# A two-layer gated cross-attention kernel on Trainium2: both fixed TensorE orders laid out anew

## The chip, the cores and the metric

The kernel runs on one core of a Trainium2 chip. A core has five engines that run at the same time, each its own stream of instructions in a fixed order: TensorE (PE, matrix products and transposes; its weight loads are a row of their own, PEld), VectorE (DVE), ScalarE (ACT), GpSimd (POOL) and SyncE (SP), which here issues most of the transfers. Data lies in SBUF (128 partitions); products are written to PSUM, which has eight banks. The metric is the device time of one execution in microseconds (us); lower is better.

## What is computed

Eight sequences (batches) of 256 rows by 512 columns pass through two layers; each layer is a gated cross-attention to a context and a gated feed-forward. Cut to what matters:

```python
x = x + tanh(g_xattn[0]) * attention0(layernorm(x), ctx)   # 16 heads of 32, causal, keys = values = ctx
x = x + tanh(g_ffn[0])   * ffn0(layernorm(x))              # ternary weights, silu(gate)*up over 2048,
                                                           # rms_norm of the result, ternary projection
x = x + tanh(g_xattn[1]) * attention1(layernorm(x), ctx)   # q and k linear + rms_norm, v linear, 16 heads,
                                                           # then an output product
x = x + tanh(g_ffn[1])   * ffn1(layernorm(x))
def ffn1(x):
    h  = x * rsqrt(mean(x*x) + EPS) * w_norm
    gv = act_quant(h) @ ternary(w_gv).T                    # act_quant: 8 bits, one scale for a row
    value, gate = split(gv)
    return x + act_quant(value * silu(gate)) @ ternary(w_out).T
```

The second scale in `ffn1` (that of `value * silu(gate)`) needs the largest value of a whole row of 2048, so nothing of the last product can start before all of a row tile's gated values are there.

## The kernel before

*Stages.* A row tile is 128 rows; there are 16, two for a batch. From 0 to about 260 us the kernel makes layer 0's ternary weights, layer 1's keys and values (kept in DRAM) and the attention of the first two batches. From about 260 to 775 us a block for each batch runs layer 0's feed-forward, and beside it the layer-0 attention of batch 2 and on, then the layer-1 attention of the first two batches, and POOL and ACT make layer 1's ternary weights. From about 799 to 1243 us a block for each batch runs layer 1's feed-forward and the layer-1 attention of the batches that follow.

*Two kinds of order.* PE's order in the last two of these stages is written out by hand: a job `at(b, (k, step))` stands at place `b + k/16` of a line of blocks, `timeline` sorts the jobs and calls them, and `pe.held` ties every product to the one before. A place is called a step in what follows (16 steps are a block of one batch, and a job at step 23.2 runs at step 7.2 of the next block). The order of DVE, ACT and POOL is not written out: it is chosen when the program is built, from a simulated timeline, and then stands fixed in the program.

*PSUM.* `pair` has two buffers, each two banks wide, shared in turn by the scores (`s`), `turned`, `back`, `nt` and `ut`. Of the rest, layer 0 has bank `o` (one buffer), `gu` (two) and `y` (one); layer 1 has `o` (one), `gu` (two) and `py` (one). A new user of a one-buffer bank waits until the last reader is done.

*Layer 0's block* (`Feed0`). `hidden` runs 32 products into `gu` for each of 8 chunks of each of two row tiles (steps 0 to 15), then ACT's tanh (`h`), two products on DVE, ACT's copy `hs`, its rest on DVE or POOL, ACT's square, and POOL's sum `acc`. `project` follows `LAG = 3` steps later with 4 products into `y`. `factor` makes the mean square of a row tile by one product `ssq` (in bank `o`) from `acc`; `add` scales `y` by it and adds it to `x`. `ready` normalises the two tiles of the next batch (`norm`) and turns them by a DMA (`xT<-yp`).

*Attention, in both layers.* `ready` normalises and turns the rows (in layer 1 also two products `lin` and their norm, for the queries). `looks` are six jobs: four `scores` (of four heads each), whose maxima DVE takes (`nm`, L415 or L407), `parts` (POOL splits the maxima into three bf16 parts, `mz` and `nmr`, ten instructions) and `shift` (PE transposes them, `nt`). `weighs` are eight jobs: `exps` (scores again, transposed, with the maxima subtracted on PE; ACT's exponentials `p`, L481) and `weigh` (products into bank `o`; ACT copies them to `oT`, L505; POOL adds up the sums, L508), in the order exps0, exps1, weigh0, exps2, weigh1, exps3, weigh2, weigh3. `done` divides by the sums and adds. Layer 0 (`Attention0.done`) transposes `oT` into `back` and the sums into bank `o`, DVE inverts them and multiplies, and adds to `x`, for both tiles in one job; the product is written back into `oT`. In layer 1 (`Attention1.done`) DVE inverts the sums (L1008), `divide` spreads them by products into `inv` (two, in banks `o` and `py`), which DVE multiplies into `oT` (L1022), and `add(i)` runs the output product `proj` (banks `o` and `py`) and adds it to `x`. L256 is the line that records every matmul, L259 every transpose.

*Layer 1's block* (`Feed1`, one object for each row tile). `first` is the batch's even tile, `second` its odd one. `ready` is `norm` (POOL and DVE make `yr`, `z`, the row's scale and the quantized `zq`; its rows are also called rs_r, y, z) and a DMA that turns it (`zT<-zq`). `glu(k)`, for k of 0 to 7, is 8 products into `gu`, and ACT's copy to `gv` (L1186); after each second one come ACT's tanh `t`, DVE's `t`, `u` and the maximum `umax`. The first tile's eight are steps 0 to 7, the second's steps 8 to 15 (there called glu 8 to 15). `done` is five jobs: `quantize` (DVE takes the maximum of `umax`, and the scale `s`, by five small instructions around L1206; ACT's two `u<-u,magic,s`, L1232; POOL's two `uq`), two DMA turns, and two `project` of eight products each into `py` (the even tile's uses bank `o`, the odd one's bank `py`), after which DVE adds the result to `x` (L1223) and it is stored to DRAM. For the very last tile `last` does the same with transposes on PE (`ut`) in place of the DMA turns.

The places of all these jobs in a block of layer 1 are the tuples of the diff's last part; steps above 16 belong to the block after the one they are counted from.

## Time and profile before

| | us |
|---|---|
| three runs | 1246.83, 1250.46, 1248.93 (median 1248.93) |
| the profiled execution | 1244.33 |
| its span, first to last instruction | 1242.6 |

| stretch of the span, us | PE busy | DVE | ACT | POOL | granted PE clock |
|---|---|---|---|---|---|
| 0 to 260: weights, keys and values, first attention | 217.25 | 191.28 | 128.69 | 92.59 | 0.91 |
| 260 to 775: layer 0's blocks | 471.16 | 284.94 | 242.30 | 251.52 | 0.99 |
| 775 to 799: hand-over | 19.70 | 17.86 | 3.56 | 20.83 | 1.00 |
| 799 to 1243: layer 1's blocks | 405.73 | 328.90 | 236.61 | 185.05 | 0.98 |

All times of the tables are of the profile's windows view; the clock is a share of full speed. PE's busy time is not time at its peak: products are pipelined, and a row of the timeline that says "x16" is sixteen of them in one stretch. In the waits view a row such as "PE inv <- DVE x: 7.4, 5, 1.7" says that PE stood idle before an `inv` product 7.4 us in all, in five waits, the longest 1.7, and that the last thing to be ready was DVE's `x`. A wait shorter than the rounding of the view, or of several causes, is put down to the one that came last. In a timeline row the columns are the start, the duration, engine, line, operation, output and inputs with their shapes, and in brackets what the instruction had waited for.

### The profile page before, as it was taken

Reading aid. Unit: us, or ns where it says so; the run is one execution under the profiler, and the core shown is the slowest. Engines: PE = TensorE matmul, PEld = TensorE weight load, DVE = VectorE, ACT = ScalarE, POOL = GpSimd, SP = SyncE. Lnnn points to the kernel's source line nnn. Section 1 sums busy time; section 2 is a strip of 40 time slices with the busy share of each in tenths; the row PEclk is TensorE's granted clock in tenths of the full one; section 3 lists DMA queues with packets and bytes.
Section 4 is the critical chain, followed back from the end, with each engine's and each line's share of the span. In section 5 each row is a group of like instructions: output and inputs, shape, how many; then the busy total and the mean of one; then the engine's idle time right before and its main releaser. Section 6 shows DMA issues by size and latency. Waiting matters only on the chain.

```text
span 1242.6 us, 29878 instructions
## 1 busy us (share of the span) xinstructions
PE 1113.8 (90%) x12466; PEld 725.7 (58%) x12565; DVE 823.0 (66%) x1776; ACT 611.2 (49%) x1108; POOL 550.0 (44%) x821
## 2 busy tenths in 40 slices
PE   7988977799999897888999998899999999999976
PEld 3444433577777666666666775455555555555553
DVE  5677797764656455375654645777777777768684
ACT  3446547356575533433344453356464645464663
POOL 3333224353343556465564424826263535424250
PEclk9998888899999998999999999999999999999998
DMA  8343424622333233223222002311212121211231
GB/s 320 127 137 114 158 85 119 221 61 96 120 99 118 64 99 82 82 70 95 84 76 66 19 18 71 109 52 31 64 35 60 35 61 35 61 35 31 39 51 43
DMA packets 101767, 103.91 MB, mean 84 GB/s; under 512 B 61312, under 2 KB 72576, under 8 KB 101632
## 3 DMA queue, kind: packets, MB, share of 16 engines
q1 hardware_dynamic: 98608, 97.01, 26.6%
q10 hardware_dynamic: 3024, 4.98, 1.3%
q8 instruction: 98, 1.61, 0.5%
q14 instruction: 37, 0.30, 0.1%
HBM read 72.09 MB, written 15.73 MB: 71 GB/s over the span
## 4 chain that ended last, share of the span: by engine, by line
PE 29%; DVE 27%; POOL 12%; ACT 8%; issue 5%; DMA 1%; POOLq 0%; DVEq 0%; ACTq 0%
PE gu L256 10%; PE o L256 5%; PE s L256 5%; DVE nm L415 4%; PE y L256 3%; PE py L256 2%; DVE u L1193 2%; DVE h L843 2%; POOL acc L850 2%; DVE ln_st L277 2%; POOL w L957 2%; DVE t L1191 2%; DVE h L842 2%; POOL q L961 2%; DVE umax L1194 2%
## 5 line engine op out<-in xcount | busy, mean ns | idle before, releaser
L256 PE MATMUL gu<-xT,gu 128*128 128x128 f16 x4096 | 254.9, 221 | 11.7 <-DVE h L843 8.3
L256 PEld LDWEIGHTS <-gu 128*128 128x128 bf16 x4096 | 237.7, 99 | 42.2 <-issue 18.6
L850 POOL TENSOR_TENSOR acc<-acc,h 128x256 f32<-128x256 f32 x112 | 83.5, 745 | 130.6 <-ACT h L848 127.0
L256 PE MATMUL gu<-gv,zT 128*128 128x256 fp8e4 x1024 | 131.4, 274 | 10.9 <-ACT gv L1186 6.4
L1186 ACT COPY gv<-gu 128x512 f32<-128x512 f32 x128 | 74.0, 585 | 116.2 <-PE gu L256 108.3
L256 PEld LDWEIGHTS <-zT 128*128 128x128 bf16 x1024 | 96.0, 98 | 57.4 <-issue 36.7
L845 ACT CAST hs<-h 128x256 f16<-128x256 f32 x128 | 51.7, 404 | 147.0 <-DVE h L843 146.6
L842 DVE SCALAR_TENSOR_TENSOR h<-h,gu 128x256 f32<-128x256 f32 x128 | 53.3, 416 | 102.3 <-ACT h L841 97.0
L256 PE MATMUL y<-pr,hs 128*128 128x512 bf16 x413 | 113.5, 383 | 6.9 <-issue 1.4
L270 POOL TENSOR_TENSOR rs_r<-rs_t,mhalf 128x1 f32<-128x1 f32 (+1 forms) x88 | 60.7, 694 | 129.0 <-DVE rs_t L268 108.1
L481 ACT ACTIVATE p<-s 128x768 f32<-128x768 f32 (+1 forms) x128 | 109.8, 908 | 15.1 <-PE s L256 15.1
L415 DVE TENSOR_REDUCE nm<-s 128x4 f32<-128x1024 f32 x64 | 75.8, 1217 | 33.9 <-PE s L256 33.9
L848 ACT ACTIVATE h<-h,hid 128x256 f32<-128x256 f32 x112 | 56.6, 507 | 70.1 <-POOL hs L295 46.6
L508 POOL TENSOR_TENSOR oT<-oT 128x256 f32<-128x256 f32 x48 | 35.3, 735 | 124.3 <-ACT oT L505 124.1
L256 PE MATMUL s<-qT,kT 32*128 32x256 f32 (+1 forms) x1024 | 78.2, 377 | 2.5 <-DVE rs_t L268 1.1
L295 POOL TENSOR_TENSOR hs<-h,hs 128x256 f16<-128x256 f32 x64 | 44.5, 695 | 77.8 <-ACT hs L845 77.8
L841 ACT ACTIVATE h<-gu 128x256 f32<-128x256 f32 x128 | 48.5, 379 | 56.9 <-PE gu L256 56.7
L1191 DVE SCALAR_TENSOR_TENSOR t<-t,gv 128x512 f32<-128x512 f32 x64 | 46.4, 725 | 41.6 <-ACT t L1190 41.6
L256 PE MATMUL s<-kT,qT 32*128 32x256 f32 (+1 forms) x1024 | 68.9, 378 | 2.0 <-DVE nm L415 1.3
L407 DVE TENSOR_REDUCE nm<-s 128x2 f32<-128x256 f32 (+1 forms) x128 | 62.9, 551 | 11.6 <-PE s L256 11.3
L256 PE MATMUL o<-p,v 128*32 128x256 f32 (+1 forms) x1024 | 64.2, 370 | 5.8 <-DVE x L1223 5.6
L256 PEld LDWEIGHTS <-hs 128*128 128x128 f16 x512 | 45.6, 101 | 35.4 <-issue 4.7
(185 smaller groups left out, 2195.4 us busy)
## 6 DMA issues: line engine op xcount, KB each, us to landing
w<-in_gvT_dram SPq DMA_DIRECT2D x32, 512.0 KB, 3.8
w<-in_guT_dram SPq DMA_DIRECT2D x32, 256.0 KB, 3.0
w<-in_outT_dram SPq DMA_DIRECT2D x16, 512.0 KB, 3.6
cT<-in_cxT_dram SPq DMA_DIRECT2D x8, 512.0 KB, 4.9
x<-in_x_dram SPq DMA_DIRECT2D x16, 256.0 KB, 6.6
kT<-in_cxT_dram SPq DMA_DIRECT2D x8, 512.0 KB, 4.0
v<-in_cx_dram SPq DMA_DIRECT2D x8, 512.0 KB, 3.8
vd<-v SPq DMA_DIRECT2D x8, 512.0 KB, 5.3
```

What stands on the lines that cost most here:

```text
L256: return self.kept(nc.tensor.matmul(*args, **kwargs))
L270: nc.gpsimd.tensor_tensor(r[:, :n], t[:, :n], mhalf[:, :n], ALU.pow)
L407: nc.vector.tensor_reduce(nm[:, :, qb], s[j][:, :, at[qb] : at[qb] + to[qb]], AX.X, ALU.max, negate=True,)
L415: nc.vector.tensor_reduce(nm, s[j].rearrange("p r (q k) -> p r q k", q=2), AX.X, ALU.max, negate=True)
L481: exp[0] = nc.scalar.activation(self.p[j], s[j][:, :, 0:n], AF.Exp)
L841: block["A"] = nc.scalar.activation(h, gu[:, 0], AF.Tanh, scale=0.5 / UP0)
L842: nc.vector.scalar_tensor_tensor(h, h, 1.0, gu[:, 0], ALU.add, ALU.mult)
L845: nc.scalar.copy(hs[:, 0], h)
L848: nc.scalar.activation(sq, h, AF.Square, scale=hid[:, 1:2])
L850: block["P"] = nc.gpsimd.tensor_tensor(self.acc[i], self.acc[i], sq, ALU.add)
L1186: nc.scalar.copy(self.gv[:, :, k % 2, :], gu)
L1191: nc.vector.scalar_tensor_tensor(t, t, 1.0, g, ALU.add, ALU.mult)
```

## The change

It is a change of order, almost without any of work. In layer 0, `factor` moves from the place ahead of chunk 6's last products to the place of chunk 7's (same step as the last `project` of a tile), `ready` of the feed-forward from 12.4, 13.4 to 11.7, 12.7; the looks are spread over steps 3.3 to 14.6 (scores at 3.3, 6.2, 9.3, 12.4), weigh1 moves from 22.2 to 21.2, and `done` becomes two jobs, each with its tile's transposes; the sums are transposed and inverted in the first; the product goes to a new tile `w`, which takes a buffer of the ring `y` (four buffers), not back into `oT`. In layer 1, `weighs(late)` swaps exps3 and weigh2; `done` becomes five jobs (invert, two `divide`, two `add`); the second `project` of `first` moves from step 18.2 to 15.4 and of `second` from 24.2 to 23.2; the looks, the weighs, `lin`, and the norms of the next feed-forward move; for the last batch but one, both `project` of `second` (tile 13) move from 23.9 to 31.9, the end of the whole order.

```diff
@@ -78,8 +78,6 @@
 MP = 3
 
 LAG = 3
-
-AHEAD0 = 1
 
 YB = 4
 
@@ -513,7 +511,7 @@
-        def weighs(self):
+        def weighs(self, late=False):
 
 
             def exps(g):
@@ -526,6 +524,8 @@
                 if g + 1 < DC:
                     steps.append(lambda g=g: exps(g + 1))
                 steps.append(lambda g=g: self.weigh(g, ps.pop(g)))
+            if late:
+                steps[5:7] = steps[6], steps[5]
             return self.counted(self.nready + DC + 2, steps)
 
         def finish(self, steps):
@@ -554,36 +554,41 @@
             return self.counted(0, [load, norm, turn])
 
         def done(self):
-            def add():
-
-                t = pair((P, 2, D), name="back")
+
+            st = {}
+
+            def divide():
                 sums = bank("o", (P, 2, P), name="sums")
                 for i in range(2):
-                    rows = slice(i * P, (i + 1) * P)
-                    for c in range(DC):
-                        pe.transpose(
-                            t[:, i, c * P : (c + 1) * P], self.oT[:, c, rows], ident
-                        )
-                    pe.transpose(sums[:, i, :], self.sums[:, rows], ident)
-                inv = small.tile([P, 2, DC, 4], F32, tag="inv", name="inv", bufs=2)
+                    pe.transpose(sums[:, i, :], self.sums[:, i * P : (i + 1) * P], ident)
+                st["inv"] = small.tile([P, 2, DC, 4], F32, tag="inv", name="inv", bufs=2)
                 nc.vector.reciprocal(
-                    inv, sums.rearrange("p i (r g e) -> p i g r e", r=4, g=DC)[:, :, :, :, 0]
+                    st["inv"], sums.rearrange("p i (r g e) -> p i g r e", r=4, g=DC)[:, :, :, :, 0]
                 )
...
-                    reach(2 * self.b + i, 1)
-
-            return self.finish([add])
+                if i == 0:
+                    divide()
+                inv = st["inv"]
+                xt = xs[2 * self.b + i]
+                w = att.tile([P, D], F32, tag="y", name="w", bufs=YB)
+                nc.vector.tensor_tensor(
+                    w.rearrange("p (h c) -> p h c", h=NH),
+                    t[:, i, :].rearrange("p (h c) -> p h c", h=NH),
+                    inv[:, i].rearrange("p g r -> p (g r)").unsqueeze(2).broadcast_to([P, NH, HD]),
+                    ALU.mult,
+                )
+                nc.vector.scalar_tensor_tensor(xt, w, tg[:, 0:1], xt, ALU.mult, ALU.add)
+                reach(2 * self.b + i, 1)
+
+            return self.finish([lambda: add(0), lambda: add(1)])
 
     def load_w(pool, name, wT):
         w = pool.tile([P, DC, D], F32, tag=f"w{name}", name=f"w{name}", bufs=1)
@@ -872,7 +877,7 @@
-                if n % 8 == 7 - AHEAD0:
+                if n % 8 == 7:
                     self.factor(n // 8)
                 self.project(n % 8, self.hs.pop(n))
                 if n % 8 == 7:
@@ -1007,19 +1012,18 @@
             def invert():
                 nc.vector.reciprocal(self.oT[:, DC + 1, :], self.sums)
 
-            def divide():
-                for k in range(2):
-                    w = bank(("o", "py")[k], (P, 2, S), name="inv")
-                    for j in range(2):
-                        pe.matmul(
-                            w[:, j, :],
-                            lhsT=spread[:, 2 * k + j, :],
-                            rhs=self.oT[:, DC + 1, :],
-                            start=True,
-                            stop=True,
-                        )
-                    cols = self.oT[:, 2 * k : 2 * k + 2, :]
-                    nc.vector.tensor_tensor(cols, cols, w, ALU.mult)
+            def divide(k):
+                w = bank(("o", "py")[k], (P, 2, S), name="inv")
+                for j in range(2):
+                    pe.matmul(
+                        w[:, j, :],
+                        lhsT=spread[:, 2 * k + j, :],
+                        rhs=self.oT[:, DC + 1, :],
+                        start=True,
+                        stop=True,
+                    )
+                cols = self.oT[:, 2 * k : 2 * k + 2, :]
+                nc.vector.tensor_tensor(cols, cols, w, ALU.mult)
 
             def add(i):
                 xt = xs[2 * self.b + i]
@@ -1029,7 +1033,7 @@
                 nc.vector.scalar_tensor_tensor(xt, t, tg[:, 1:2], xt, ALU.mult, ALU.add)
                 reach(2 * self.b + i, 3)
 
-            return self.finish([invert, divide, lambda: add(0), lambda: add(1)])
+            return self.finish([invert, *(lambda f=f, k=k: f(k) for f in (divide, add) for k in range(2))])
 
     att1 = [Attention1(b) for b in range(B)]
     x2 = ctx.enter_context(tc.tile_pool(name="x2", bufs=1, side="right", reuse_waits="tile"))
@@ -1058,24 +1062,24 @@
 
 
 
-        jobs += at(0, *zip((-5.0, -4.0), feed0[0].ready()), (-4.5, *att0[1].done()))
+        jobs += at(0, *zip((-5.0, -4.0), feed0[0].ready()), *zip((-4.5, -4.4), att0[1].done()))
         for b in range(B):
             jobs += at(b, *((k, step) for k, step in enumerate(feed0[b].chunks())))
             if b == 0:
                 jobs += at(b, *zip((4.4, 5.4), feed0[1].ready()))
             elif b + 1 < B:
-                jobs += at(b, *zip((12.4, 13.4), feed0[b + 1].ready()))
+                jobs += at(b, *zip((11.7, 12.7), feed0[b + 1].ready()))
         for n, a in enumerate([*att0[2:], *att1[:2]]):
             if n < B - 2:
                 jobs += at(n, (-11.0, lambda n=n: rows(n + 2)))
-                jobs += at(n, *zip((-4.8, -2.4, 4.2 if n == 0 else 0.2), a.ready()))
+                jobs += at(n, *zip((-4.8, -2.4, 4.2 if n == 0 else 1.2), a.ready()))
             else:
-                jobs += at(n, *zip((-9.6, -7.6, -4.8, -3.7, -2.6, -2.5, 0.2), a.ready()))
-            jobs += at(n, *zip((*((5.4, 7.2) if n == 0 else (1.2, 5.2)), 9.2, 10.4, 10.8, 14.6), a.looks()))
+                jobs += at(n, *zip((-9.6, -7.6, -4.8, -3.3, -2.4, -2.3, 1.2), a.ready()))
+            jobs += at(n, *zip((*((5.4, 7.2) if n == 0 else (3.3, 6.2)), 9.3, 12.4, 12.6, 14.6), a.looks()))
             if a is not att1[1]:
-                jobs += at(n, *zip((15.3, 18.2, 19.2, 20.2, 22.2, 23.2, 24.2, 25.2), a.weighs()))
+                jobs += at(n, *zip((15.3, 18.2, 19.2, 20.2, 21.2, 23.2, 24.2, 25.2), a.weighs()))
             if n < B - 2:
-                jobs += at(n, (27.7, *a.done()))
+                jobs += at(n, *zip((26.6, 27.6), a.done()))
         pe.held = True
         timeline(*jobs)
     w0ctx.close()
@@ -1281,24 +1285,25 @@
         end = b == B - 1
         jobs += at(b, *((k, step) for k, step in enumerate(first.glus() + second.glus())))
 
-        far = {B - 1: (15.9, 15.9), B - 2: (15.95, 15.95), B - 3: (13.2, 17.3)}.get(b, (13.2, 18.2))
+        far = {B - 1: (15.95, 15.95), B - 2: (15.95, 15.95)}.get(b, (13.2, 15.4))
         jobs += at(b, *zip((7.4 if b == B - 2 else 8.6, 9.6, 9.8, *far), first.done()))
         if end:
             jobs += at(b, (16.0, second.last))
         else:
-            far = {B - 2: (23.9, 23.9), B - 3: (21.2, 22.2)}.get(b, (21.2, 24.2))
+            far = {B - 2: (31.9, 31.9), B - 3: (21.2, 22.2)}.get(b, (21.2, 23.2))
             jobs += at(b, *zip((17.4, 18.4, 18.6, *far), second.done()))
         if b >= 2:
 
-            late = 15.6 if b == 2 else 16.2
-            jobs += at(b - 3, *zip((3.6, 12.2, 12.5, 14.2, late, 16.5, 18.9), a.ready()))
-            jobs += at(b - 2, *zip((4.4, 6.4, 7.4, 9.3, 10.4, 14.1), a.looks()))
+            head = b == 2
+            turn, far = (11.25, 15.6) if head else (12.3, 17.2)
+            jobs += at(b - 3, *zip((3.6, turn, 12.5, 14.2, far, 17.5, 20.3), a.ready()))
+            jobs += at(b - 2, *zip((5.3, 7.3, 9.2, 11.3, 11.6, 14.1), a.looks()))
         if b >= 1:
-            steps = (-0.8, 0.6, 2.3, 2.5, 3.2, 3.4, 4.2, 5.0) if end else (-0.8, 1.2, 3.2, 3.4, 4.2, 5.6, 6.2, 7.2)
-            jobs += at(b - 1, *zip(steps, a.weighs()))
-        steps = (5.1, 6.9, 7.6, 8.2) if end else (7.3, 9.2, 10.2, 11.2)
+            steps = (-0.8, 0.6, 2.3, 2.5, 3.2, 3.4, 4.2, 5.0) if end else (-1.1, 0.2, 2.2, 3.2, 4.2, 6.2, 6.3, 8.2)
+            jobs += at(b - 1, *zip(steps, a.weighs(not end)))
+        steps = (5.1, 6.9, 6.9, 7.6, 8.2) if end else (8.3, 11.1, 11.15, 11.2, 12.2)
         jobs += at(b - 1, *zip(steps, a.done()))
-        for n, f in zip((7.7, 8.4) if end else (10.3, 13.0), (first, second)):
+        for n, f in zip((7.7, 8.4) if end else (11.35, 14.0), (first, second)):
             norm, turn = f.ready()
             jobs += at(b - 1, (n, norm), (n + 1.7, turn))
     timeline(*jobs)
```

What the change does to the other engines' order shows in the built programs, listed here for a steady block of layer 1 (numbers are the glu's; `oT(w3)` is the copy of the last weigh). ACT, from the last weigh on:

```text
before: oT(w3), gv7, u x2, gv8, t, gv9, gv10, t, ...
after:  gv7, t7, gv8, u x2, oT(w3), gv9, t9, gv10, gv11, t11, gv12, xT
```

DVE, from the first scores of the block on:

```text
before: nm x2, t, u, umax, reciprocal oT, amax, nm, amax, nm, s8i, s.., x<-py, oT*inv x2, t, u, ...
after:  nm x2, x<-py, t, u, umax, nm, amax, nm, amax, s8i, s, g, s, nm, t, reciprocal oT, nm, u, t,
        oT*inv, umax, oT*inv, u, umax, x<-proj
```

PE, jobs by glu step of the block, after (before: exps3 in step 5, weigh2 in 6, weigh3 in 7, `divide` in 9 beside the fourth scores, `add` in 10 and 11):

```text
14.9 exps0 | 0 exps1 | 1 lin1 | 2 weigh0 | 3 exps2 | 4 weigh1, turned | 5 py (second, 8 of 16), scores0
6 weigh2, exps3 | 7 py (second), scores1 | 8 weigh3 | 9 scores2 | 11 inv x2, proj0, scores3
12 proj1, turned y | 13 py (first, 8 of 16) | 14 nt, lin0 | 15 py (first)
```

POOL before has the parts (`mz`, `nmr`) of a batch together, ahead of the norm's y and z; after, the second norm's `rs_r`, `yr`, `z` stand ahead of and among them. In a block of layer 0, POOL before has the ten parts together and ahead of the norms' y; after, the norms' rs_r and y stand ahead of and among them. DVE there, after, from `ssq` of the second tile on:

```text
after:  nm x4, q, rs_t<-ssq, h, h, rgf, x<-y, reciprocal, hs, w, x, h, bn_stats, h, w, bn_aggr, x, h, bn_stats x3, h, ...
        nm x2 (the last maxima)
```

More of the change, by code (lines that the diff above doesn't have):

```diff
@@ L569, in add @@
                 nc.vector.reciprocal(
-                    inv, sums.rearrange("p i (r g e) -> p i g r e", r=4, g=DC)[:, :, :, :, 0]
+                    st["inv"], sums.rearrange("p i (r g e) -> p i g r e", r=4, g=DC)[:, :, :, :, 0]
                 )
-                for i in range(2):
-                    xt = xs[2 * self.b + i]
-                    w = self.oT[:, 2 * i : 2 * i + 2, :].rearrange("p c t -> p (c t)")
-                    nc.vector.tensor_tensor(
-                        w.rearrange("p (h c) -> p h c", h=NH),
-                        t[:, i, :].rearrange("p (h c) -> p h c", h=NH),
-                        inv[:, i].rearrange("p g r -> p (g r)").unsqueeze(2).broadcast_to([P, NH, HD]),
-                        ALU.mult,
-                    )
-                    nc.vector.scalar_tensor_tensor(
-                        xt, w, tg[:, 0:1], xt, ALU.mult, ALU.add
-                    )
-                    reach(2 * self.b + i, 1)
@@ L586, in done, with add @@
-            return self.finish([add])
+            def add(i):
+                if i == 0:
+                    st["t"] = pair((P, 2, D), name="back")
+                t = st["t"]
+                for c in range(DC):
+                    pe.transpose(
+                        t[:, i, c * P : (c + 1) * P], self.oT[:, c, i * P : (i + 1) * P], ident
+                    )
+                if i == 0:
+                    divide()
[10 more added lines that the diff above has]
+                reach(2 * self.b + i, 1)
@@ L1008, in invert @@
                 nc.vector.reciprocal(self.oT[:, DC + 1, :], self.sums)
-            def divide():
-                for k in range(2):
-                    w = bank(("o", "py")[k], (P, 2, S), name="inv")
-                    for j in range(2):
-                        pe.matmul(
-                            w[:, j, :],
-                            lhsT=spread[:, 2 * k + j, :],
-                            rhs=self.oT[:, DC + 1, :],
-                            start=True,
-                            stop=True,
-                        )
-                    cols = self.oT[:, 2 * k : 2 * k + 2, :]
-                    nc.vector.tensor_tensor(cols, cols, w, ALU.mult)
+            def divide(k):
[10 more added lines that the diff above has]
+                nc.vector.tensor_tensor(cols, cols, w, ALU.mult)
             def add(i):
```

## The prediction

> **What bounds the kernel now.** I read the page first (busy shares), then who waited for whom on TensorE (PE) in two stretches, then the timelines of VectorE (DVE) and ScalarE (ACT) in one block of layer 1, then the granted clock in short windows.
>
> ```profile
> span 1242.6 us, 29878 instructions
> PE 1113.8 (90%) x12466; PEld 725.7 (58%) x12565; DVE 823.0 (66%) x1776; ACT 611.2 (49%) x1108; POOL 550.0 (44%) x821
> ```
>
> PE is busy 90% of the span, and each engine runs its instructions in a fixed order. So the change cannot remove work from PE; it can only shorten or lengthen the holes in PE's row, 129 us in all. The waits of PE from 290 to 760 us (layer 0's feed-forward; columns: total us, times, longest):
>
> ```profile
> PE ssq L256 <- POOL acc L853: 6.8, 3, 3.6
> PE gu L256 <- DVE h L843: 6.3, 5, 1.6
> PE ssq L256 <- ACT oT L505: 5.5, 4, 2.3
> PE s L256 <- ACT p L481: 4.3, 7, 0.7
> PE gu L256 <- DMA xT<-yp: 3.3, 3, 1.6
> PE turned L259 <- ACT p L481: 2.0, 1, 2.0
> PE turned L259 <- POOL acc L850: 1.8, 1, 1.8
> PE back L259 <- DVE nm L407: 1.7, 3, 1.1
> ```
>
> The mean square `ssq` is the costliest single place (12.3 us). From 880 to 1180 us, five equal blocks of layer 1 (one and the same `s` product starts at 937.94 and 998.16, so a block lasts 60.2 us):
>
> ```profile
> PE inv L256 <- DVE x L1223: 7.4, 5, 1.7
> PE o L256 <- DVE x L1223: 4.5, 4, 1.2
> PE lin L256 <- DVE lin L696: 2.7, 4, 0.9
> PE gu L256 <- DMA zT<-zq: 1.2, 3, 0.5
> ```
>
> The first two are the one-buffer banks `py` and `o`: the next user waits until DVE has stored the feed-forward's product. The four make 15.8 us, 3.2 a block. What lies around them on DVE and ACT:
>
> ```profile
> 943.53 1.74 DVE L1008 RECIPROCAL oT<-oT 128x256 f32<-128x256 f32 x1
> 945.21 1.21 DVE L415 TENSOR_REDUCE nm<-s 128x4 f32<-128x1024 f32 x1
> 948.03 0.75 DVE L1223 SCALAR_TENSOR_TENSOR x<-py,g,x 128x512 f32<-128x512 f32 x1
> 948.69 0.68 DVE L1022 TENSOR_TENSOR oT<-oT,inv 128x512 f32<-128x512 f32 x1
> ```
> ```profile
> 942.05 0.59 ACT L505 COPY oT<-o 128x512 f32<-128x512 f32 x1 [0.61 <-PE o L256]
> 944.02 0.59 ACT L1186 COPY gv<-gu 128x512 f32<-128x512 f32 x1 [1.39 <-PE gu L256]
> 948.15 2.37 ACT L1232 ACTIVATE u<-u,magic,s 128x1024 f32<-128x1024 f32 x2 [3.54 <-DVE s L1206]
> ```
>
> The reader is to see the order: ACT copies the last `oT` and a `gv` before it waits 3.54 us for the quantizing scale `s`, and DVE's reciprocal is long done when PE comes to `inv`.
>
> **The change, part by part.**
>
> *Layer 1, what it removes.* `second`'s products end in step 23.2, not 24.2, so bank `py` is stored long before `inv`; `first`'s end in 15.4, not 18.2, three steps before the first weigh needs bank `o`; the two `lin` are three steps apart, not two; between the first `proj` and the next block's first `gu` PE now has some 17.9 us of work (before 15.7), so `zT` lands in time. All 3.2 us a block, for the six blocks with this order 19 us.
>
> *Layer 1, what it adds.* In the changed program's own order (listed in the section above) ACT's two `u` now stand ahead of the last `oT` and of glu 9's `gv`, and DVE's reciprocal behind `s` and behind `t` of glus 8 and 9. I add the chain up, from the end of `second`'s last products (step 7), by the rows of the timelines: DVE x 0.75; t, u, umax 3 x 0.69; nm 1.2, amax 0.1, nm 1.2; five small ones to `s` 0.7: 6.0 us. ACT u 2.37, oT 0.59, gv 0.59, tanh 0.72: 10.3. DVE t 0.69, reciprocal 1.74: 12.7. Only then can `inv` start. PE's own work in between: s 1.08, gu 0.98, weigh 1.86, gu 0.98, s 1.08, two gu 1.76: 7.7. So 5.0 us of wait, part of it already ahead of glu 11, because the `gu` bank has two buffers and glu 9's copy is stuck behind `u`. After the reciprocal DVE has nm 1.2, u 0.69, t 0.69 and the first multiplication 0.68 to do, 3.2 us; PE has 2.0 us of `inv`, then `proj` waits 1.2 (before, a whole glu stood between them). Together 6.2 us a block, 37 us in six; net of the 19 removed: +18. Queued behind ACT's wait for `s` are the last weigh's copy, POOL's sum of it and the two quantized halves `uq`; behind DVE's, the maxima of the third scores.
>
> *The clock.* Short matmuls between waits also cost clock:
>
> ```profile
> 1203.00:1206.00 3.00, 1.03 (x8) 1.00 0.22 44
> 1206.00:1209.00 3.00, 1.86 (x8) 0.52 0.66 126
> ```
>
> (columns: us, PE busy, granted clock.) After waits of 1.14 and 1.71 us around one `gu` the clock fell to half, and the 16 `py` after it took 5.46 us against 3.62 elsewhere: 1.84 lost. The other end is none: waits of 2.85 and 0.99 around 773 to 777 us left it at 1.00. The changed block has the first pattern (2.4, 2.3 and 1.2 us around 0.9 and 2.0 of work), so I take 1.8 a block, +11. The Trainium skill says otherwise: "TensorE: Matmul & The Clock Gate", in "Why this matters for your kernels", asks only that no single idle gap exceeds about 3 us. By it the clock would stay whole here and the sum below would be 11 us smaller; the row at 1206 has no gap above 1.8 us and fell all the same, so the row decides.
>
> *Layer 1, the last pair of batches.* The turned maxima `nt` come 7.9 us of PE work after the last scores; DVE and POOL need about 9 for them (nm 2.4, the first tile's norm rows 959 to 964 in between, parts 1.8). +2, between 0 and 4.
>
> *Layer 0.* In the first half of a block the scores stand a whole weigh behind the exponentials and `ssq` stands behind scores and 32 products, so `s<-p` 4.3 and `ssq<-oT` 5.5 go: -10. In the second half `ssq` of the second tile moves behind 32 more products and a `y` (2.0 + 0.85), which covers 2.9 of its longest wait of 3.6. But the fourth scores move from four steps ahead of `nt` to two. From the step of `ssq` on, DVE has, ahead of these last maxima: nm 1.95, q 0.70, three h pairs 2.7, x 0.75, inverse 0.35, hs 0.41, two w 1.3, two x 1.9, four bn_stats 2.5, small ones 0.9: 13.5; with q 0.7, its own nm 1.95 and some 1.2 of waiting it ends at 17.3. POOL then owes, in its new order, the norms' y (two pairs, 1.51 each), rs_r, acc 0.72, hs 0.67 and the parts (some 2.1): `mz` is done at about 21 without layer 1's weight quantizing beside it and 23.4 with it. PE is there at 17.2. So `nt` waits 3.8 twice and 6.2 twice, 20 us; the waits this absorbs (ssq 6.8, gu<-h 6.3, xT 3.3, turned 3.8, back 1.7) are 21.9. With one more fall of the clock (+2) and crumbs (+1): layer 0 gives -9. Ends: -20 if POOL lets the parts through, 0 if the absorbed waits come back.
>
> *Splitting `done` in two and its new tile `w`.* Same instructions, same sizes; `w` takes a buffer of ring `y`, whose other users are steps away. Nothing, hidden behind the 32 products between the halves (2.0 us against w 0.65 + x 0.95); without that cover 1.6 a block. Layer 0's first stage has the same products in slightly other order: 0. The hand-over at 773 us: `ssq` one `y` later, -1.
>
> *The end.* Tile 13's 16 products leave the place at 1208 to 1214.5 (0.95 wait, 5.46) for the hole ahead of the last transposes:
>
> ```profile
> 1231.58 1.26 PE L259 MATMUL ut<-ident_b,uq 128*128 128x128 bf16 x8 [3.87 <-DVE uq L1263]
> ```
>
> That saves 6.3. But DVE's store of them now stands ahead of the last t, u, umax: from the last gu, py 3.6 + x 0.75 + 2.07 + small 0.9 + ACT 0.73 + uq 0.43 = 8.5, against 7.3 before: +1.2, and 0.6 for ACT, which is nearly full there. -4.5, between -6 and 0.
>
> **The sum.** +18 +11 +2 -9 -1 -4.5 = +16.5. On the profiled execution, span 1242.6 and 1244.33 in all, that is 1260.8; the median of the runs lies 4.6 above it, 1248.93, so 1265.
>
> **The rivals.** *Faster:* the chain through `s` does not bind. Then layer 1 keeps its 19 us and pays only the wait of `proj` for the multiplication next to it (0.5 a block, 3); with layer 0, hand-over and end -14.5: -30, 1219. For it: DVE is idle 3 to 4 us a block (939.12 came after 3.43 of idling), so a store that comes a little earlier moves the whole chain. Against it: the order on ACT and DVE is fixed, and the chain has 5 us too much. It decides from where the new waits, clock and all, fall below 5.3 a block (3.2 removed, 12.5 gained elsewhere over six). *No change:* the chain holds, but the clock stays whole and layer 0 gives 15, its middle to good end: 18 + 2 - 15 - 1 - 4.5 = 0, 1249. *Slower still, by layer 0:* the waits of `nt` (over 3 us each) let the clock fall every time and `xT` is late as before; layer 0 gives nothing or loses: +28 to +35, about 1280. For it: 488 to 492 us, where 32 products took 3.62 us after a wait of 2.75. Against: the pause lets DVE and POOL catch up. *The change doesn't do what it says:* the weighing steps are even on PE alone; that is the forecast itself.
>
> **How the numbers follow.** Forecast 0.58, faster 0.20, no change 0.12, slower still 0.10. A difference of 0.3% (3.7 us) is about what runs of this kernel can tell. Ends of the costs: low, chain 1 us shorter and no clock +12, layer 0 -20, end -6, hand-over -1: -15, 1234; high, chain 1 us longer with clock +35, last pair +4, nothing elsewhere: +39, 1288. I leave out the outermost on both sides: 1236 to 1283.
>
> **What would show it.** In a block of layer 1: `inv` waiting for the reciprocal (L1010 or near) 2 us or more, a `gu` waiting for `gv` just before, `proj` waiting for DVE 1 us; ACT's `u` followed by the last `oT`; no wait of `o` or `inv` for x. In layer 0: no `ssq<-oT`, `nt` waiting for POOL's `mz` 3 to 6 us four times. At the end: no hole of 3.87. I am wrong if blocks of layer 1 last under 60 us.

## The result, and the profile after

The changed kernel takes 1324.15 us (median of four runs, 1323.47 to 1326.02), the kernel before 1247.88 beside it: a ratio of 1.0614 with a 95% interval of 1.0588 to 1.064. It is slower by 76 us, some 60 more than I had forecast. The first lines of the page of its profile:

```profile
span 1322.5 us, 29890 instructions
PE 1157.2 (88%) x12473; PEld 751.1 (57%) x12565; DVE 817.6 (62%) x1776; ACT 611.4 (46%) x1108; POOL 545.7 (41%) x821
```

DVE, ACT and POOL work about as long as before (823.0, 611.2, 550.0). PE's busy time grows by 43.4 us with the same products, and its holes by 36.5. The granted clock also falls more often: summed over windows of 1 us from 240 us to the end, what the clock lacks of full speed (1 less the granted share, times the time) is 13.7 us before, in 5 falls, and 58.0 after, in 23.

To place the loss I cut every span at the first product of layer 0's feed-forward (`gu<-xT`), at that of layer 1's (`gu<-gv`), and at the last store's sum:

| us | up to layer 0's first product | layer 0's blocks and hand-over | layer 1 to the last store |
|---|---|---|---|
| before | 232.7 | 566.5 | 439.7 |
| after | 240.7 | 585.2 | 492.8 |
| difference | +8.0 | +18.7 | +53.1 |

PE's busy time and holes in the last two columns, here to the end of the span, tell two losses of different kinds. In layer 0 the holes grow by 13.3 us (50.4 to 63.7) and the busy time by 5.5 (516.1 to 521.5); the clock lacks 16.3 us more there (25.2 against 8.9), but all four of its falls between 350 and 570 us begin while PE stands, so what it lacks is more than what it costs. In layer 1 the holes grow by 16.3 us (37.8 to 54.1) and the busy time by 36.8 (405.7 to 442.5); the clock lacks 25.9 us more (32.7 against 6.8), which leaves 10.9 of busy time that it does not account for.

The waits of PE in layer 0's part of the changed kernel (290 to 780 us):

```profile
PE nt L257 <- POOL mz L432: 27.5, 4, 8.7
PE s L254 <- DVE nm L405: 4.8, 10, 0.7
PE lin L254 <- DVE rs_t L266: 3.8, 1, 3.8
PE sums L257 <- DVE rs_t L266: 3.7, 3, 1.6
PE lin L254 <- DVE nm L413: 3.0, 1, 3.0
```

The old waits of `ssq` are gone from the list. In their place stands `nt`, four times 6.9 us on average, and behind it new names (`lin`, `sums`). One of the four, in the timeline of DVE, POOL and PE:

```profile
488.33 1.01 DVE L405 TENSOR_REDUCE nm<-s 128x2 f32<-128x256 f32 x2
489.65 1.51 POOL L288 TENSOR_SCALAR y<-x,ln_mv,rs_r 128x512 f32<-128x512 f32 x2
...
491.83 1.95 POOL L288 TENSOR_SCALAR y<-x,ln_mv,rs_r 128x512 f32<-128x512 f32 x2
493.75 0.61 POOL L425 TENSOR_SCALAR mz<-nm 128x16 bf16<-128x16 f32 x2
...
497.45 0.37 POOL L432 TENSOR_SCALAR mz<-nmr 128x16 bf16<-128x16 f32 x2
497.71 0.46 PE L257 MATMUL nt<-ident_b,mz 128*128 128x128 bf16 x2 [8.73 <-POOL mz L432]
```

The last maxima were done at 489.3. POOL made the norm's two pairs of `y` first and came to the parts 4.4 us later; the parts then took 4.1, and PE stood 8.73.

In layer 1, 900 to 1260 us, which holds five waits of `inv`:

```profile
PE inv L254 <- DVE oT L1013: 10.6, 5, 2.1
PE gu L254 <- ACT gv L1190: 9.7, 5, 1.9
PE s L254 <- ACT p L479: 8.1, 6, 2.1
```

The four lines of before (`inv` and `o` for `x`, `lin`, `zT`) are gone, as meant. The first two lines here are the chain of the prediction. One instance of it, DVE, ACT and PE in order of time:

```profile
1066.60 0.15 DVE L1210 TENSOR_TENSOR s<-s,back 128x1 f32<-128x1 f32 x1
1066.78 2.38 ACT L1236 ACTIVATE u<-u,magic,s 128x1024 f32<-128x1024 f32 x2 [3.21 <-DVE s L1210]
...
1069.06 0.56 ACT L503 COPY oT<-o 128x512 f32<-128x512 f32 x1
1069.53 0.58 ACT L1190 COPY gv<-gu 128x512 f32<-128x512 f32 x1
...
1071.50 1.75 DVE L1013 RECIPROCAL oT<-oT 128x256 f32<-128x256 f32 x1
...
1073.30 2.07 PE L254 MATMUL inv<-oT,spread 128*128 128x256 f32 x4 [2.11 <-DVE oT L1013]
```

ACT waits 3.21 us for the scale `s`, runs both `u`, and only then copies the last weigh; PE stands 1.93 for `gv` and 2.11 for the reciprocal. The third line, `s` for `p`, I had not seen coming. ACT alone, some 40 us earlier:

```profile
1020.30 0.58 ACT L1190 COPY gv<-gu 128x512 f32<-128x512 f32 x1 [1.22 <-PE gu L254]
1029.93 0.63 ACT L702 ACTIVATE junk<-lin 128x512 bf16<-128x512 f32 x1 [9.04 <-DVE lin L701]
1030.55 1.92 ACT L479 ACTIVATE p<-s 128x1024 f32<-128x1024 f32 x2
```
```profile
1026.22 0.69 DVE L1149 TENSOR_REDUCE amax<-z 128x1 f32<-128x512 f32 x1 [1.09 <-POOL z L1147]
...
1028.78 0.52 DVE L1154 TENSOR_SCALAR z<-z,s 128x512 f32<-128x512 f32 x1
1029.22 0.68 DVE L701 TENSOR_TENSOR lin<-lin,rqb 128x512 f32<-128x512 f32 x1
```

ACT idles 9.04 us before the square of `lin` (the sum of squares for the queries' norm), and the block's first exponentials are queued behind it. The square waits for DVE's bias sum of `lin` (L701), which stands in DVE's order behind the quantizing of the second norm (L1149 to L1154), although PE's product `lin` was done at 1024.2. The scores that want the exponentials' buffers wait 2.08 us, and the clock falls:

```profile
1029.00:1032.00 3.00, 0.92 (x7) 0.95 0.19 38
1032.00:1035.00 3.00, 3.00 (x25) 0.50 0.03 6
1035.00:1038.00 3.00, 3.00 (x12) 0.50 0.23 87
```

(stretch, its length, PE busy, granted clock, DMA share, GB/s.) For six microseconds PE is busy all the time at half speed. From 860 to 1180 us before, no window of 1 us fell below 0.99; after, 25.5 us are lacking between 861 and 1175.

### The profile page after: what moved, and what is told of

It reads as the page before. It is cut to its first block, busy times and chain, and to the rows that moved or that the text cites. A ratio compares the mean times of both kernels' runs of the same rounds, so it can differ in the third digit from the quotient of the medians.

```text
span 1322.5 us, 29890 instructions
## 1 busy us (share of the span) xinstructions
PE 1157.2 (88%) x12473; PEld 751.1 (57%) x12565; DVE 817.6 (62%) x1776; ACT 611.4 (46%) x1108; POOL 545.7 (41%) x821
## 4 chain that ended last, share of the span: by engine, by line
PE 33%; DVE 24%; POOL 13%; ACT 9%; issue 4%; DMA 0%; DVEq 0%; POOLq 0%; ACTq 0%
PE gu L254 11%; PE s L254 5%; PE o L254 4%; PE y L254 3%; PE proj L254 3%; DVE ln_st L275 3%; DVE h L848 2%; PE py L254 2%; DVE nm L413 2%; POOL rs_r L268 2%; PE lin L254 2%; DVE h L847 2%; PE inv L254 2%; POOL w L962 2%; POOL q L966 2%
## 5 line engine op out<-in xcount | busy, mean ns | idle before, releaser
L254 PE MATMUL gu<-xT,gu 128*128 128x128 f16 x4096 | 260.2, 224 | 3.6 <-DVE h L848 3.6
L254 PEld LDWEIGHTS <-gu 128*128 128x128 bf16 x4096 | 243.6, 100 | 31.7 <-issue 16.9
L254 PE MATMUL gu<-gv,zT 128*128 128x256 fp8e4 x1024 | 135.7, 280 | 18.7 <-ACT gv L1190 17.4
L479 ACT ACTIVATE p<-s 128x768 f32<-128x768 f32 (+1 forms) x128 | 109.8, 908 | 12.7 <-PE s L254 12.7
L254 PE MATMUL s<-qT,kT 32*128 32x256 f32 (+1 forms) x1024 | 89.2, 387 | 13.1 <-ACT p L479 10.2
L1237 POOL TENSOR_SCALAR uq<-u 128x1024 bf16<-128x1024 f32 x30 | 31.3, 1045 | 131.3 <-ACT u L1236 130.2
L413 DVE TENSOR_REDUCE nm<-s 128x4 f32<-128x1024 f32 x64 | 76.3, 1211 | 2.8 <-PE s L254 2.8
L254 PE MATMUL lin<-wq,xT 128*128 128x512 f32 x128 | 65.3, 657 | 8.2 <-DVE rs_t L266 4.2
L254 PEld LDWEIGHTS s<-qT,kT 32*128 32x128 f32 x1024 | 50.0, 192 | 38.9 <-ACT p L479 14.1
```

The lines of the kernel that those rows point to most:

```text
L254: return self.kept(nc.tensor.matmul(*args, **kwargs))
L413: nc.vector.tensor_reduce(nm, s[j].rearrange("p r (q k) -> p r q k", q=2), AX.X, ALU.max, negate=True)
L479: exp[0] = nc.scalar.activation(self.p[j], s[j][:, :, 0:n], AF.Exp)
```

## The experiments

Every ratio below is against the kernel before in the same session, with its 95% interval. The names e1 to e17 are used from here on.

**e1 and e2: one layer's part each.** e1 takes from the change the places of the last stage, `weighs(late)` and `Attention1.done`; e2 takes all the rest (mean square, looks, `ready`, `Attention0.done`).

> The kernel before with only the change's layer-1 places and its split divide. If the two layers' parts simply add up (as the traces suggest: +52 us over layer 1's blocks, -5 at the end), about 1296 us. If layer 1's loss comes from layer 0 ending in another state (what is left over at the hand-over), it is under 1270.

> The kernel before with only the change's layer-0 part (mean square, looks, split done with its new tile). If the parts add up: +8 us before the first products into gu, +21 by the hand-over, so about 1278 us. My prediction had -10 for all of it (1239). If it is over 1290, layer 0's part also harms layer 1.

Measured: e1 1296.15 us (1.0395, 1.0363 to 1.0427), e2 1275.2 (1.0231, 1.0205 to 1.0256). 49.3 and 28.3 add to 77.6; the whole change was 76.3. The two layers can be studied apart, and both parts lose.

**e3, e4, e5: the two queues of layer 1.** PE's order is left as changed in e3, and only one tie is added:

```diff
-  nc.scalar.copy(self.oT[:, g : behind + 1 : behind - g], o)
+  copied[0] = nc.scalar.copy(self.oT[:, g : behind + 1 : behind - g], o)
...
-  behind(nc.scalar.activation(u, u, AF.Identity, bias=magic, scale=sc), exp[0])
+  behind(behind(nc.scalar.activation(u, u, AF.Identity, bias=magic, scale=sc), exp[0]), copied[0])
```

> The changed kernel, with ScalarE's two u of the quantizing ordered behind the copy of the last weigh; PE's order is the same. If the chain u, last oT, reciprocal makes the wait of inv, that wait (2.1 us a block) and the fall of the clock after it (3.4) go in most blocks: 1295 to 1305 us. Rival, PE's own order is too tight there and the gu's wait for gv (1.9) only grows: 1318 or more.

In e4 the second norm's reduction is tied behind `lin`'s bias sum:

```diff
-  nc.vector.tensor_tensor(t, out, bias(), ALU.add)
+  added[0] = nc.vector.tensor_tensor(t, out, bias(), ALU.add)
...
-  nc.vector.tensor_reduce(amax, z, AX.X, ALU.max, apply_absolute_value=True)
+  behind(nc.vector.tensor_reduce(amax, z, AX.X, ALU.max, apply_absolute_value=True), added[0])
...
-  for n, f in zip((7.7, 8.4) if end else (11.35, 14.0), (first, second)):
+  for n, f in zip((7.7, 8.4) if end else (11.35, 14.3), (first, second)):
```

> The changed kernel, with VectorE's bias sum of the first lin ordered ahead of the second norm's quantizing (that norm is issued at 14.3, not 14.0), so that the square of lin no longer holds the first exponentials back on ScalarE. If that queue makes the wait of 2.1 us before the second scores of the block and the fall of the clock after it, both go: 5.5 us in five blocks, about 1297 us. Rival, only the wait goes and the clock falls all the same: about 1314. Rival, the second norm becomes late: no gain.

> The changed kernel with both orders of e3 and e4 (u behind the last copy on ScalarE, lin's sum ahead of the second norm on VectorE). If they mend two separate waits: 25 + 23 us, so about 1276. If one only uncovers the other: 1285 or more.

Measured: e3 1298.81 (1.0414, 1.0383 to 1.0446), e4 1301.27 (1.0439, 1.0411 to 1.0467), e5 1279.87 (1.0257, 1.0226 to 1.0287). Each gives what was worked out from its one wait and the falls of the clock behind it (-25 and -23), and together 44 of the 48. The waits of PE, 900 to 1260 us, in e3, where the reciprocal is early, and in e4, where the exponentials are:

```profile
PE s L254 <- ACT p L480: 8.3, 7, 2.1
PE gu L254 <- ACT gv L1191: 7.7, 6, 1.7
PE proj L254 <- DVE oT L1027: 5.1, 5, 1.1
```
```profile
PE gu L254 <- ACT gv L1191: 10.7, 7, 1.9
PE inv L254 <- DVE oT L1014: 9.2, 5, 2.1
```

In e3 no `inv` waits any more; what comes up in its place is the wait of `proj` for the multiplication next to it, 1.1 a block, and `s` for `p` is untouched. In e4 it is the other way round: `p` is gone, the chain is whole. Two separate queues, then. With both mended, layer 1 takes 444.9 us against 492.8, and from 861 to 1175 us the clock does not fall.

**e6 and e7: the wait of `nt` in layer 0.** Both start from e5. e6 moves two places; e7 leaves PE's order and changes POOL's:

```diff
-  (3.3, 6.2)), 9.3, 12.4, 12.6, 14.6), a.looks())
+  (3.3, 6.2)), 9.3, 10.4, 10.8, 14.6), a.looks())      # e6
...
-  nc.gpsimd.tensor_scalar(y, t, mv[:, i, 0:1], r[:, i : i + 1], ALU.add, ALU.mult)
+  behind(nc.gpsimd.tensor_scalar(y, t, mv[:, i, 0:1], r[:, i : i + 1], ALU.add, ALU.mult), last)   # e7
...
-  jobs += at(b, *zip((11.7, 12.7), feed0[b + 1].ready()))
+  jobs += at(b, *zip((12.65, 12.7), feed0[b + 1].ready()))   # e7; last is the parts' last instruction
```

> e5 with layer 0's fourth scores and the parts of the maxima back at 10.4 and 10.8 (change: 12.4, 12.6); GpSimd then makes the parts ahead of the norm's two y. If the two steps between the last scores and nt cost all of the wait of nt (27.5 us and 15 us of clock more than before): about 1237. Rival, the waits that nt absorbed (sums of squares, xT, h) come back: 1256 to 1266.

> e5 with PE's order kept and only the feed-forward norm issued at 12.65 and its two y ordered behind the parts on GpSimd. If GpSimd's order makes the wait of nt (my prediction's step: the parts behind the y), the wait falls from 6.9 to some 3 each and part of the clock returns: about 1260. Rival, VectorE's maxima are what is late (done at 489.3 where PE is ready at 489.0) and the parts take 4 us anyway: 1268 or more.

Measured: e6 1258.27 (1.0085, 1.0057 to 1.0114), e7 1269.23 (1.0172, 1.0138 to 1.0206). The time of e6 is the rival's: it is 21.6 us faster than e5, not 42. But the waits that come up are, for the most part, not those that the rival named. From 280 to 800 us:

```profile
PE back L257 <- DVE nm L407: 14.7, 5, 4.1
PE s L254 <- DVE nm L407: 6.4, 11, 1.1
PE ssq L254 <- POOL acc L860: 4.4, 3, 2.0
```

`nt` is gone from it, and `back`, the transposes of `done`, waits instead: the first half of the split `done` (26.6, which is step 10.6 of the next block) now comes right behind the last scores (10.4), and its pair buffer is free only when DVE has taken their maxima. In e7 the same view reads

```profile
PE nt L257 <- POOL mz L435: 9.8, 8, 3.0
```

So POOL's order, with the norm issued a little later, makes 17.7 of the 27.5 us of `nt` (e5 has the 27.5 too); the rest goes with how late the maxima and their parts are, for in e6, with the scores early, `nt` does not wait. The time, though, is in the range of e7's rival: 10.6 us less than e5. The other waits of PE grew, from 24.3 us to 33.8 in that stretch, so half of what `nt` lost stands before other products. My first theory for e6, that the two steps cost everything, fell.

**e8 and e11: the 8 us before layer 0.** In the first stage PE's order is not written by hand. e8 starts from e5 and calls both halves of the first attention's `done` as one job; e11 starts from e6 and also puts all eight `back` transposes ahead of the sums, as before the change, with the product still in `w`:

```diff
+            def whole():
+                st["t"] = pair((P, 2, D), name="back")
+                for i in range(2):
+                    for c in range(DC):
+                        pe.transpose(st["t"][:, i, c * P : (c + 1) * P], self.oT[:, c, i * P : (i + 1) * P], ident)
+                divide()
+                for i in range(2):
+                    add(i, True)      # without its own transposes
```

> e5 with the first attention's split done called as one job in the first stage, where the order is not written by hand. If that split makes the 8 us by which the first products into gu come late: about 1267. Rival, the first stage's delay has another source (the built order moved by later stages): 1276.

> e6 with all eight transposes of the first attention's done ahead of its sums, as before the change, but with the product still in the new tile w. If the 8 us before layer 0 come from the second half's transposes standing late in the order that the build chooses: 1250 us, first products into gu at 233. Rival, they come from w taking a buffer of ring y: 1258, first gu at 240.

Measured: e8 1277.65 (1.0242, 1.0209 to 1.0274), first product of layer 0 at 240.1; e11 1256.75 (1.0084, 1.0058 to 1.011), first product at 234.2. Joining the jobs does nothing, because the second half's transposes are still issued behind the division and the build still lets other products pass them: they start at 152.4 in e8 and at 152.8 in the changed kernel, but the last two at 146.4 in the kernel before and 146.5 in e11. Issuing them first brings 7 of the 8 us back, so the tile `w` is not the cause. But the total falls by 1.5 us only, less than the scatter of the runs, and against the kernel before the two are alike (1.0084 and 1.0085). In the profiles layer 0 took 571.2 us against 568.7. Where the rest of the early start went, I did not find out.

**e9, e10, e14: the parts that were meant to gain.** All on the kernel before: the mean square alone, tile 13 alone, both.

```diff
-                if n % 8 == 7 - AHEAD0:      # e9, e14
+                if n % 8 == 7:
...
-            far = {B - 2: (23.9, 23.9), B - 3: (21.2, 22.2)}.get(b, (21.2, 24.2))      # e10, e14
+            far = {B - 2: (31.9, 31.9), B - 3: (21.2, 22.2)}.get(b, (21.2, 24.2))
```

> The kernel before with the mean square alone moved (factor at chunk 7). My prediction let this part take away most of the 12.3 us of waits at ssq. If that holds by itself: 1238 to 1243 us. Rival, the wait only moves to the next y, whose one bank now stays taken until the scale is there: 1247 or more.

> The kernel before with tile 13's two halves of the last product alone moved to 31.9. Prediction's term: -4.5 (between -6 and 0), so about 1244 us. Rival, VectorE's store of it delays the last tile by as much: 1248.

> The kernel before with the mean square moved (e9) and tile 13 at the end (e10). If these two add: 1247.5 - 3 - 5.5, about 1239. So if layer 1's even places are worth something once mended, e13 is 2 to 5 us below this one; if their loss lay in the places, e13 is above it.

Measured: e9 1244.45 (0.9977, 0.9962 to 0.9992), e10 1241.77 (0.9952, 0.9928 to 0.9977), e14 1239.63 (0.9946, 0.9929 to 0.9964). Tile 13 gains what was worked out, though e10's runs scatter widely (1234 to 1247; its interval allows 3 to 9 us). The mean square gains 2.9 us, between my two cases: from 290 to 760 us its 12.3 us of waits are gone, but those of `s` for `p` grow from 4.3 to 8.7 and those of `gu` for `h` from 6.3 to 7.4; all waits there sum to 31.9 us, against 35.0.

**e12 and e13: layer 1's even steps, mended.** e12 is e6 with

```diff
-  (7.4 if b == B - 2 else 8.6, 9.6, 9.8, *far), first.done()
+  (7.4 if b == B - 2 else 9.4, 10.2, 10.4, *far), first.done()
...
-  else (8.3, 11.1, 11.15, 11.2, 12.2)
+  else (8.3, 11.1, 11.15, 12.1, 13.1)
...
-  for n, f in zip((7.7, 8.4) if end else (11.35, 14.3), (first, second)):
+  for n, f in zip((7.7, 8.4) if end else (12.2, 14.3), (first, second)):
```

and the two `u` also tied behind the last `gv` copy issued. e13 puts that layer 1 on the kernel before with e9's mean square.

> e6 with one glu between the spread sums and each output product (12.1, 13.1), first's quantizing at 9.4, and on ScalarE the two u also behind glu 9's copy. If the waits left in layer 1's blocks (gu for gv 1.7, proj for the multiplication 1.1) are those two orders: 2.4 us in six blocks less, 1244. Rival, the quantized tile or the next norm becomes late: 1258 or more.

> The kernel before with the mean square moved (as e9) and layer 1 of e12 (the change's places, with the three orders mended and proj one glu later). If stages add up: first gu-to-hand-over of e9 (-3) and layer 1 of e12 (432.9 us against 439.7): about 1236 us. If layer 1's mending only worked after e12's layer 0: 1243 or more.

Measured: e12 1245.48 (0.9987, 0.9974 to 1.0001), e13 1236.05 (0.9928, 0.9899 to 0.9956). e13's waits, 880 to 1180 us, where the kernel before had 15.8 us in four lines:

```profile
PE s L254 <- DVE nm L416: 2.7, 6, 0.5
PE s L254 <- DVE nT L446: 1.5, 1, 1.5
PE turned L257 <- DVE nm L416: 1.1, 2, 0.6
```

Layer 1 takes 432.9 us against 436.1 in e14, which has the places of before and tile 13 at the end, and the medians are 3.6 us apart. So the even steps, with the orders off PE mended, are worth some 3 us, and cost 57 as they were built (492.8). Not run: the three ties with the places of before, so how much of the 3 us is the places' own is not shown.

**e15, e16, e17: layer 0's places one by one.** e15 is e13 with the first half's scores spread; e16 and e17 each add one more piece of the change to e15.

```diff
-  (1.2, 5.2)), 9.2, 10.4, 10.8, 14.6), a.looks())
+  (3.3, 6.2)), 9.2, 10.4, 10.8, 14.6), a.looks())      # e15, with the queries' turn at 1.2, not 0.2
+  (3.3, 6.2)), 9.3, 12.1, 12.6, 14.6), a.looks())      # e16, with the feed-forward's ready at 11.8, 12.7
...
-  jobs += at(n, (27.7, *a.done()))
+  jobs += at(n, *zip((26.6, 27.6), a.done()))      # e17, with the split done and its tile w
```

> e13 with layer 0's first two scores at 3.3 and 6.2 and the turn of the queries at 1.2, as in the change; the last two stay at 9.2 and 10.4. Prediction's term: the waits of the scores for the exponentials (8.7 us in e9) go, so 5 to 10 us under e13. Rival, VectorE then has three maxima in a row and the waits move to back and nt: no gain or a loss.

> e15 with layer 0's last scores, parts and feed-forward norm late as in the change (12.1, 12.6; norm at 11.8), done as before. If the wait of nt belongs to these places alone: four waits of 3 to 7 us and the falls of the clock after them, 1236 to 1256 us. Rival, nt is late only together with the split done, whose two products and sums stand ahead of the maxima on VectorE: under 1230.

> e15 with the change's split done (26.6, 27.6 and -4.5, -4.4; new tile w). If its earlier first half, right behind the last scores at 10.4, makes e12's waits of back for the maxima (16.6 us) and the 8 us of the first stage: about 1241. If the split is harmless: 1226 or less.

Measured: e15 1221.02 (0.9802, 0.9775 to 0.9829), e16 1258.56 (1.0106, 1.0078 to 1.0133), e17 1242.61 (0.9973, 0.9957 to 0.9989). Spreading the first two scores gains 15 us, more than the 5 to 10 expected: layer 0 goes from 565.0 to 552.8, of the 8.4 us that `s` waited for `p` in e13, 1.3 are left, and the clock lacks 6.2 us less there. e16 adds 37.5 us, a little more than expected (its scores stand at 12.1 and its norm at 11.8, where the change has 12.4 and 11.7); its waits from 240 to 790 us begin with

```profile
PE nt L257 <- POOL mz L435: 25.4, 8, 5.8
PE y L254 <- DVE x L895: 7.3, 5, 2.0
```

so the late last scores, with the norm ahead of them, make `nt` wait without any help of the split `done`. e17 adds 21.6 us and has e6's line again:

```profile
PE back L257 <- DVE nm L408: 14.8, 5, 4.1
```

Its first product of layer 0 comes at 241.7, against 231.6 in e15: 10.1 of its loss lie in the first stage, and layer 0 takes 14.9 us more. The two prices do not add. Layer 0 takes 36.5 us more in e16 and 14.9 in e17, which on e15's 552.8 would make 604; e5, which has both, takes 586.7. Where the last scores are late, `back` does not stand behind them. e15 beats both kernels, by 2.0% the one before. The first lines of its page:

```profile
span 1220.7 us, 29965 instructions
PE 1122.2 (92%) x12565; PEld 727.0 (60%) x12565; DVE 822.8 (67%) x1776; ACT 608.2 (50%) x1108; POOL 545.0 (45%) x821
```

## Why the prediction was wrong

The direction and the first mechanism were right; the time lies outside the range. By the stages of the table, layer 0 with the hand-over was to gain 10 us and lost 18.7, layer 1 with the end was to lose 26.5 and lost 53.1, and the first stage was put at 0 and lost 8.0.

*Layer 1, the chain through `s`* was right as told (ACT's `u` ahead of the last copy, the reciprocal behind it), and e3 shows it by taking it away. Its size was 6.2 us a block; measured are 2.1 at `inv` and 1.9 at `gu`, and nothing at `proj`, whose 1.2 appears only where the reciprocal is early (e3: 1.1). The step that I left out is ACT's other queue: I followed the last weigh's copy and not the first exponentials, which stand behind `lin`'s square (2.1 us at most, e4). All waits of PE in the stretches shown sum to 31.0 us after and 17.1 before, which is 2.8 a block over five blocks, close to the 3.0 that I had (6.2 less 3.2): that was luck, one error hid the other.

*The clock* is the step that failed in layer 1. It was priced at one fall of 1.8 us a block, by the row at 1206. From 861 to 1175 us, four and a half blocks, it lacks 25.5 us, 5.7 a block: the pair of waits at `gu` and `inv` brings one fall, the wait behind `lin`'s square another, and a fall takes 1.7 or 3.4 us. A block lasts 70.2 us (the odd tiles' stores from 963.99 to 1174.65 over three) against 60.2: 2.8 from waits, some 5.7 from the clock, 1.5 not accounted for. Over the whole of layer 1, 11 us were forecast; the clock lacks 25.9 more than before, and PE's busy time grows by 36.8. Some 7 of the 10.9 that the clock leaves go with the places: e13, which has nearly the same ones and lacks the 6.8 us of before, keeps PE busy for 412.9 us, against 405.7. Why, no run shows.

*Layer 0, the waits of `nt`*: 27.5 us against 20 (5.4, 5.7, 7.7 and 8.7 against twice 3.8 and twice 6.2), and the reason is as predicted (DVE's late maxima, then the norm's `y` ahead of the parts on POOL; e7 and e16). The old waits went as forecast, too: of `ssq`, `h`, `p`, `xT`, `turned` and `back` 31.7 us in the kernel before, 1.6 are left. The step that failed is that I took `nt` for the only new wait, with 1 us for all the rest. Outside `nt` the changed kernel still waits 22.4 us in that stretch (49.9 in all, where before had 35.0): `s` for `nm` 7.5 in place of 1.3, `lin` 6.8, `sums` 3.7 and smaller ones. Those of `lin` stand in e16 as well (4.8 and 4.1), without the split `done`; where those of `sums` come from, no run takes apart. So PE's holes, which were to shrink by 12 us with the hand-over, grew by 13.3. The clock lacks 22.1 us from 280 to 800, against 6.8, where I had +2, but PE's busy time grew by 5.5 only. Two pieces inside it were right: the first half's spread gains (e15: 15 us; my 10 held 4.3 for `s` for `p` and 5.5 for `ssq`), and the mean square's waits are covered, though they are worth 2.9 us only (e9).

*Splitting `done`* I put at nothing, hidden behind the 32 products between its halves. In e17 it costs 21.6 us, of which 14.9 in layer 0: I asked whether the second half is covered and not whether the first half's buffer is free at its earlier place. In the changed kernel, with its late last scores, that wait of `back` is not on the list, so this price is not a part of its +18.7 as it stands. *The first stage* I put at 0, since "the same products" stand there; but its order is chosen at build time, and the split moved it: +8.0.

*The end* was right: -4.5 forecast, -5.5 alone (e10), -4.8 beside the mean square (e14 against e9). The hand-over, the last pair and the earlier weigh1 of layer 0 were not tried by themselves.

*The rivals.* "Faster" was to win where the new waits of layer 1, clock and all, stay below 5.3 a block; they came to 6.2 (31.0 over five) and 5.7. "Slower still, by layer 0" had the right mechanism, `nt` with a fall of the clock each time, and was given 0.10 with layer 1 as forecast; both layers failing in one direction was in none of the cases, which is why the range ended at 1283.

## What to carry to other kernels

When one engine's order is written by hand and the others' is chosen at build time, a move is priced by walking each of the other engines' new orders in full and asking of every instruction that a product waits for what stands ahead of it; the first such queue found is not the last. Mend the queue before giving up the places: here three ties between instructions, with `proj` a glu later and the quantizing and a norm later too, turned layer 1's steps from 57 us of loss into 3 of gain. And where one new wait is priced, the products behind it want a price as well: here the wait that was foreseen came to 27.5 us, and those that were put at 1 us to some 17.

## What the runs showed of the hardware

The granted clock falls to half in units: behind the first stage, what a fall lacks sums to 1.7, 3.4 or 5.1 us, in every fall of all these runs that does not run into the end. In the changed kernel it fell nine times between 900 and 1260 us, where no wait of PE is longer than 2.1 us. The Trainium skill, "TensorE: Matmul & The Clock Gate", section "Why this matters for your kernels", asks for no idle gap over about 3 us; these rows show that waits of 2 us with little work between them are enough. In e5, where those waits are gone or down to 1.7, there is no fall from 861 to 1175 us. The length of the longest wait does not settle it either: in e13 the clock falls at 1142.8, behind a single wait of 1.46 us (`s` for `nT`) that has short products around it.

Where a fall happens to lie also scatters the stages: e15, e16 and e17 share layer 1's places, and it takes 432.5, 430.2 and 428.5 us, with 6.8, 1.7 and 0.3 us of clock lacking in it. Layer 0 scatters more: in e10 DVE, ACT and POOL run the same instructions there in the same order as in the kernel before, and it takes 572.8 us against 566.5, with 17.3 us of clock lacking against 8.9. A difference of that size in one stage of one profile is no evidence of anything else.
